# Four graph layers on one core: the closing algebra of layer 3 cut up by chunk, and artanh written as two logarithms

## The chip, the core and the metric

The kernel runs on one core of one Trainium2 chip. The metric is the device time of one execution in microseconds (us). The profiles below are taken from one execution each; in them PE is TensorE, DVE is VectorE, ACT is ScalarE, POOL is GpSimd and SP is SyncE.

## What is computed

Input `x` has 4096 nodes of 64 features, `adj` is a 4096 x 4096 matrix of zeros and ones. Four layers follow one another, each of the form x + layer(relu(layernorm(x)), adj). The change concerns the last layer, a graph layer in hyperbolic space:

```python
def _artanh(x):
    return jnp.arctanh(jnp.clip(x, -ARTANH_BOUND, ARTANH_BOUND))

def mobius_scalar_mul(r, x):
    x_norm = _norm(x)
    return _tanh(r * _artanh(x_norm)) * (x / x_norm)

def weighted_midpoint_lincomb(A, X):
    gamma = lambda_x(X)
    num = A @ (gamma * X)
    den = A @ (gamma - 1.0)
    sgn = jnp.where(den >= 0.0, 1.0, -1.0)
    den = sgn * jnp.maximum(jnp.abs(den), DEN_EPS)
    two_mean = num / den
    mid = mobius_scalar_mul(0.5, two_mean)
    alpha = jnp.sum(A, axis=1, keepdims=True)
    return mobius_scalar_mul(alpha, mid)

# layer 3: XW = mobius_matvec(W, h); AXW = weighted_midpoint_lincomb(A, XW)
#          x + expmap0(relu(logmap0(AXW)))
```

So after the large product with A, every node needs a sign, a length, an artanh, a tanh and a scaling of its 64 numbers.

## The kernel before

**Tiling.** The 4096 nodes are 32 blocks of 128. For layer 3 the output is made in 8 chunks (`u` = 0 to 7) of four blocks (CB = 4, 512 nodes). `sum3` (line 1674) runs the product for one chunk: for each of its four blocks, matmuls over the input blocks, each with 196 columns (65 numbers in three bf16 parts, and a column of ones). The sums lie in PSUM, for most chunks in two banks of two blocks each (pool `one`, four banks), for chunks 5 and 2 in one double bank (pool `two`).

**Order of layer 3.** `layer3` (line 1690) first sums what is available of the inputs: chunks 0, 1, 2 over the first half of the blocks, taken out into SBUF as `early`; then chunks 3, 4, 5 over the first half. When the last quarter of the inputs is there, it finishes chunks 3, 4, 5, then 0, 1, 2, and then makes 6 and 7 whole. After each chunk `take3` (line 1737) brings the sums out: ScalarE copies the first part and the column of ones (`alpha`), VectorE adds the two other parts, and for chunks 0 to 2 the `early` part. Then `summed` (line 1729) collects chunks: once three are together, or at once for the chunks 6 and 7 (`alone=True`), it hands them to `post3`.

**The closing algebra.** `post3` (line 1757) works on three chunks at a time, 12 numbers per partition in the small steps, or on one chunk with 4. It has two sections. The head, once for each chunk, takes the sign (`sgn`), multiplies the 256 numbers by it (written as `n` in the profile, from the tile's name `n65`), squares them on ScalarE (`sq`) and on VectorE (the positive part), makes `den` in two steps and reduces the squares to `ss`. The rest is for all chunks of the group together: `preload(AF.Ln)`, the reciprocal `rc` of `den`, the root in `lengths` (names `guess`, `nt`, `nu`, `ny`, `norm`), `t`, then `artanh2` (line 1595), the multiplication by `alpha`, tanh on ScalarE, and for each chunk a scaling of `n`, the addition to `X` and the output DMA, issued by SyncE.

**artanh2.** The argument is clipped (`axc`). VectorE makes 1 - x (`at`), its reciprocal (`rc`) and (1 + x) times that; ScalarE takes the logarithm, and `preload(AF.Tanh)`, an activation on a constant, brings in the table of tanh. Meanwhile VectorE evaluates a polynomial (`flow`, `x`, `po`) that replaces the logarithm for arguments under 0.25. `artanh2` is called four times by `post3` and four times by `pre3` (line 1621), which prepares the inputs of layer 3.

**What sets the order.** Each engine runs its instructions in the order in which the program issues them. The class `Weave` (line 605) decides that order when the program is built: it keeps a planned clock for each engine with estimated durations. Generators such as `post3` yield their VectorE (`DV`), ScalarE (`AC`) and SyncE (`SY`) steps; they lie in `weave.work`, and the first two of them are looked at (`width` is 2). `draw` (line 711), called after every fourth matmul in `sum3`, issues each VectorE or ScalarE step whose planned end lies no later than TensorE's planned time plus a margin (`LAG` 0.4 us and `late`, 1.0 us since layer 1), the first generator first. `fill` (line 692) does that ahead of an instruction of `take3`, which is issued directly. `force` issues whatever can begin first, and `finish`, after the last chunk, forces all that is left. Just before `finish`, `layer3` loads a register of each engine from the tile `flag`, by which a general program would run if the adjacency matrix were not made of zeros and ones.

**Buffers.** Small tiles (`stat`) share 22 buffers of 24 columns, those of up to 512 columns (`b2`) share 20.

Of the kernel before, what the change touches and what calls it, by code (L numbers as in the profile page):

```python
# [12 lines left out]
AF = mybir.ActivationFunctionType  # L13
ALU = mybir.AluOpType
AX = mybir.AxisListType
# [4 lines left out]
D = 64  # L20
# [9 lines left out]
DEN_EPS = 1e-10  # L30
# [541 lines left out]
CB = 4  # L572
# [219 lines left out]
def fast_kernel(ctx: ExitStack, tc: tile.TileContext, t: dict, out: bass.AP, flag: bass.AP):  # L792
# [24 lines left out]
    weave = Weave()  # L817
# [11 lines left out]
    def b2(name, shape=(P, QB, D), dtype=F32):  # L829
        return b2p.tile(list(shape), dtype, tag="b2", name=name)  # L830

    def stat(name, n):
        return small.tile([P, ST], F32, tag="st", name=name)[:, :n]
# [3 lines left out]
    DV, AC, GP, SY = (Engine(weave, x.e, x.real, True) for x in (V, S_, G_, Y_))  # L837
# [79 lines left out]
    def rows(s, width=D):  # L917
        return s[:, :, None].to_broadcast([P, s.shape[1], width])
# [12 lines left out]
    def recip(v):  # L931
        r = stat("rc", v.shape[1])
        yield DV.reciprocal(r, v)
        return r
# [160 lines left out]
    ones = const.tile([P, 1], F32, name="fones")  # L1095
# [483 lines left out]
    def lengths(s):  # L1579

        yield DV.tensor_scalar(s, s, NORM_EPS2, None, op0=ALU.max)
        r = yield from rsqrt(s)
        n = stat("norm", s.shape[1])
        yield DV.tensor_tensor(n, s, r, ALU.mult)
        return n, r
# [5 lines left out]
    def preload(func):  # L1591

        yield AC.activation(void, tab, func)

    def artanh2(x, between=()):

        nb = x.shape[1]
        xc = stat("axc", nb)
        yield DV.tensor_scalar(xc, x, ARTANH_BOUND, None, op0=ALU.min)
        r = stat("at", nb)  # L1600
        yield DV.tensor_scalar(r, xc, -1.0, 1.0, op0=ALU.mult, op1=ALU.add)
        q = yield from recip(r)
        yield DV.scalar_tensor_tensor(q, xc, 1.0, q, op0=ALU.add, op1=ALU.mult)
        yield AC.activation(q, q, AF.Ln)
        yield from preload(AF.Tanh)
        low = small.tile([P, ST], I32, tag="st", name="flow")[:, :nb]
        yield DV.tensor_scalar(low, xc, 0.25, None, op0=ALU.is_lt)
        x2, p = stat("x2", nb), stat("po", nb)
        yield DV.tensor_tensor(x2, xc, xc, ALU.mult)
        yield DV.tensor_scalar(p, x2, *(2.0 * c for c in ARTANH_POLY[:2]), op0=ALU.mult, op1=ALU.add)  # L1610
        yield DV.tensor_tensor(p, p, x2, ALU.mult)
        for c in ARTANH_POLY[2:-1]:
            yield DV.scalar_tensor_tensor(p, p, 2.0 * c, x2, op0=ALU.add, op1=ALU.mult)
        yield DV.scalar_tensor_tensor(p, p, 2.0 * ARTANH_POLY[-1], xc, op0=ALU.add, op1=ALU.mult)
        yield from between
        yield DV.copy_predicated(q, low, p)
        return q
# [3 lines left out]
    def pre3(q, kind):  # L1621
# [15 lines left out]
        mr, c = r[:, QB:], stat("ratio", QB)  # L1637
        yield DV.tensor_tensor(c, n[:, QB:], r[:, :QB], ALU.mult)
        a = yield from artanh2(n[:, :QB])
        yield DV.scalar_tensor_tensor(a, a, 0.5, c, op0=ALU.mult, op1=ALU.mult)  # L1640
        yield DV.tensor_scalar(a, a, TANH_CLAMP, None, op0=ALU.min)
# [48 lines left out]
    def layer3():  # L1690
# [21 lines left out]
        for place, u in enumerate(sets[1]):  # L1712
            sum3(u, place, half + QB if place < 2 else half, NB)
            summed(u, take3(u))
        for place, u in enumerate(sets[0]):
            sum3(u, place, half, NB)
            summed(u, take3(u, early.pop(u)))
        for place, u in enumerate((6, 7)):
            sum3(u, place, 0, NB)
            summed(u, take3(u), alone=True)  # L1720
# [3 lines left out]
        weave.finish()  # L1724
        return others

    group = []

    def summed(u, parts3, alone=False):
        group.append((u, parts3))  # L1730
        if alone or len(group) == 3:
            weave.add(post3(group[:]))
            group.clear()

    out_nm = out

# [17 lines left out]
            V.tensor_tensor(alpha, alpha, more[1], ALU.add)  # L1754
        return n65, alpha

    def post3(parts3):

        nb = CB * len(parts3)
        sgn, den, ss = stat("sgn", nb), stat("den", nb), stat("ss", 2 * nb)
        part = [slice(i * CB, (i + 1) * CB) for i in range(len(parts3))]
        vs = [n65[:, :, :D] for u, (n65, al) in parts3]
        for h, v, (u, (n65, al)) in zip(part, vs, parts3):
            d = n65[:, :, D]
            yield DV.tensor_scalar(sgn[:, h], d, 0.0, 2.0, op0=ALU.is_ge, op1=ALU.mult)
            yield DV.scalar_tensor_tensor(v, rows(sgn[:, h]), -1.0, v, op0=ALU.add, op1=ALU.mult)  # L1770
            sq = b2("sq")
            yield AC.activation(sq[:, :CB, :], v, AF.Square)
            yield DV.scalar_tensor_tensor(sq[:, CB:, :], v, 0.0, v, op0=ALU.max, op1=ALU.mult)
            yield DV.tensor_scalar(den[:, h], d, -1.0, DEN_EPS, op0=ALU.mult, op1=ALU.max)
            yield DV.tensor_tensor(den[:, h], den[:, h], d, ALU.max)
            yield DV.tensor_reduce(ss.rearrange("p (k b) -> p k b", k=2)[:, :, h],
                                   sq.rearrange("p (k b) d -> p k b d", k=2), AX.X, ALU.add)
        yield from preload(AF.Ln)
        rd = yield from recip(den)
        n, r = yield from lengths(ss)  # L1780
        t = stat("t", nb)
        yield DV.tensor_tensor(t, n[:, :nb], rd, ALU.mult)
        ratio = stat("ratio", nb)

        def between():
            yield DV.tensor_tensor(ratio, n[:, nb:], r[:, :nb], ALU.mult)

        a = yield from artanh2(t, between())
        for h, (u, (n65, al)) in zip(part, parts3):
            yield DV.scalar_tensor_tensor(a[:, h], a[:, h], 0.25, al, op0=ALU.mult, op1=ALU.mult)  # L1790
        yield DV.scalar_tensor_tensor(a, a, ARTANH_MAX, ratio, op0=ALU.min, op1=ALU.mult)
        yield AC.activation(a, a, AF.Tanh)
        yield DV.tensor_tensor(a, a, r[:, nb:], ALU.mult)
        for h, v, (u, (n65, al)) in zip(part, vs, parts3):
            yield DV.scalar_tensor_tensor(v, v, 0.0, rows(a[:, h]), op0=ALU.max, op1=ALU.mult)
            x = X[u // 2][:, (u % 2) * CB:(u % 2 + 1) * CB, :]
            yield DV.tensor_tensor(x, x, v, ALU.add)
            yield SY.dma_start(out_nm[:, u * CB:(u + 1) * CB, :], x)
# [103 lines left out]
```

## Time and profile before

| | us |
|---|---|
| median of 3 runs | 809.76 (808.28 to 809.77) |
| the profiled execution | 808.12 |
| its span, first to last instruction | 806.1 |

Mean granted clock of TensorE: 0.992. In stretches of layer 3's end, busy us of each engine:

| stretch | PE | DVE | ACT |
|---|---|---|---|
| 718.10 to 740.70 | 22.60 | 16.59 | 10.90 |
| 740.70 to 750.30 (sums of 3, 4, 5 end) | 9.60 | 2.33 | 1.40 |
| 750.30 to 766.60 (chunks 0, 1, 2) | 16.30 | 14.52 | 6.10 |
| 766.60 to 777.40 (chunk 6) | 10.80 | 10.01 | 3.41 |
| 777.40 to 788.30 (chunk 7) | 10.90 | 9.72 | 4.38 |
| 788.30 to 806.10 (after the last matmul) | 0.01 | 10.46 | 6.04 |

A line of the timeline gives start, duration, engine, line, operation, output and input by the program's names with their shapes, and how many instructions are merged in it; in brackets stands how long the engine was idle before, and what released it. All steps issued through `DV` and `AC` have the line of the helper, 781, so they are told apart by their names. Consecutive VectorE instructions overlap by up to 0.1 us, so the sum of durations is larger than the time they take.

### The profile page before, as it was taken

The numbers are of one execution on the slowest core, as the hardware profiler recorded it, in microseconds if no ns is written. First come the engines' busy times: TensorE is split into PE (matmuls) and PEld (weight loads), VectorE is DVE, ScalarE is ACT, GpSimd is POOL, SyncE is SP. The second block draws the span as 40 slices with busy tenths as digits, with TensorE's granted clock in tenths as the row PEclk, the third lists the DMA queues.
The fourth block names the chain that finished last, engine by engine and source line by source line (L and its number), as shares of the span: only waits on it lengthen the run. The fifth ranks groups of instructions, "written<-read, shape, count | busy, mean of one in ns | idle before, by whom it ended". The sixth has DMA issues, their size and how long they took to land. (4 is left out here: it accounts for less than half of the span.)

```text
span 806.1 us, 12128 instructions
## 1 busy us (share of the span) xinstructions
PE 772.6 (96%) x4494; PEld 360.1 (45%) x4494; DVE 635.6 (79%) x1429; ACT 397.8 (49%) x613; POOL 60.6 (8%) x125
## 2 busy tenths in 40 slices
PE   5999999999999999999999999999999999999991
PEld 2334444544443323333333333444444444599991
DVE  6886867877778798888888887878788777776696
ACT  5655555566556556667666664122220245444332
POOL 3332232231000000000000000000000000000000
PEclk9999999999999999999999999999999999999996
DMA  9999999999601032004022016597888600000010
GB/s 221 152 177 191 215 163 211 202 180 205 186 26 40 0 103 85 23 8 124 0 66 66 0 51 229 193 338 240 292 307 280 216 7 20 2 1 2 2 41 17
DMA packets 43955, 98.40 MB, mean 122 GB/s; under 512 B 5104, under 2 KB 20464, under 8 KB 43888
## 3 DMA queue, kind: packets, MB, share of 16 engines
q1 hardware_dynamic: 25888, 78.98, 29.0%
q0 software_dynamic: 15840, 14.42, 19.1%
q10 hardware_dynamic: 2160, 4.14, 1.4%
q8 instruction: 37, 0.61, 0.3%
q14 instruction: 30, 0.25, 0.1%
HBM read 135.54 MB, written 5.24 MB: 175 GB/s over the span
## 5 line engine op out<-in xcount | busy, mean ns | idle before, releaser
L781 ACT ACTIVATE sig<-score,fatt_add,fatt_mul 128x1024 f32<-128x1024 f32 x128 | 148.3, 1200 | 85.2 <-PE score L976 84.1
L781 DVE TENSOR_TENSOR sig<-sig,A 128x1024 f32<-128x1024 f32 x128 | 151.6, 1222 | 38.2 <-ACT sig L781 37.5
L781 DVE SCALAR_TENSOR_TENSOR whole<-whole 128x1024 f32<-128x1024 f32 x128 | 153.0, 1219 | 6.7 <-DMA whole<-in_adjT 6.1
L781 ACT ACTIVATE w<-cnt 128x512 int16<-128x512 f32 x198 | 111.6, 595 | 88.4 <-PE cnt L976 83.7
L976 PE MATMUL score<-qd,kT 64*128 64x512 f32 x512 | 128.2, 617 | 0.0
L976 PE MATMUL acc<-sig,S 128*64 128x512 f32 x512 | 125.4, 606 | 1.5 <-DVE sig L781 1.4
L976 PE MATMUL acc<-A,hm 128*128 128x512 fp8e4 x512 | 115.9, 379 | 0.0
L976 PEld LDWEIGHTS <-hm 128*128 128x128 bf16 x768 | 73.4, 98 | 91.3 <-issue 9.8
L976 PE MATMUL cnt<-A,ftri 128*128 128x512 fp8e4 x256 | 98.0, 386 | 8.1 <-ACT A L781 8.1
L976 PE MATMUL cnt<-A,fupd 128*128 128x512 fp8e4 x248 | 95.4, 385 | 3.4 <-ACT w L781 0.9
L976 PE MATMUL acc<-S,A 128*128 128x196 bf16 x1024 | 88.2, 246 | 0.2 <-DVE mx L781 0.2
L976 PEld LDWEIGHTS <-A 128*128 128x128 fp8e4 x1024 | 87.1, 96 | 1.5 <-issue 1.2
L976 PEld LDWEIGHTS score<-qd,kT 64*128 64x128 f32 x512 | 43.7, 186 | 80.9 <-ACT sig L781 39.1
L976 PE MATMUL acc<-w,hm 128*128 128x512 bf16 x256 | 75.6, 379 | 0.0
L781 DVE TENSOR_SCALAR w<-cnt 128x512 int16<-128x512 f32 x58 | 40.1, 691 | 39.4 <-PE cnt L976 38.2
L860 POOL DMA_DIRECT2D A<-in_adjT x110 | 58.8, 536 | 133.1 <-DMA A<-in_adjT 132.3
L976 PEld LDWEIGHTS acc<-sig,S 128*64 128x64 f32 x512 | 30.4, 136 | 82.7 <-issue 38.8
L976 PEld LDWEIGHTS <-lo 128*64 128x64 bf16 x768 | 39.3, 109 | 51.2 <-issue 22.5
L976 PE MATMUL acc<-A,lo 128*64 128x512 fp8e4 x512 | 59.4, 381 | 0.0
L781 ACT ACTIVATE mt<-acc 64x512 f32<-64x512 f32 x32 | 18.9, 591 | 66.0 <-PE acc L976 65.5
L976 PEld LDWEIGHTS <-ftri 128*128 128x128 bf16 x256 | 24.8, 98 | 47.2 <-issue 20.3
L1659 POOL MEMSET S<- 128x4 bf16 x8 | 0.9, 115 | 533.6 <-PE ps_l L976 463.2
(185 smaller groups left out, 631.5 us busy)
## 6 DMA issues: line engine op xcount, KB each, us to landing
whole<-in_adjT SPq DMA_DIRECT2D x128, 512.0 KB, 6.9
A<-in_adjT POOLq DMA_DIRECT2D x110, 128.0 KB, 14.0
qd<-qs SPq DMA_DIRECT2D x16, 128.0 KB, 4.1
mx<-gs SPq DMA_DIRECT2D x16, 128.0 KB, 7.8
xT<-gs SPq DMA_DIRECT2D x8, 256.0 KB, 7.2
x<-in_x SPq DMA_DIRECT2D x6, 256.0 KB, 6.2
xs<-x SPq DMA_DIRECT2D x4, 256.0 KB, 6.0
qs<-qT ACTq DMA_DIRECT2D x4, 256.0 KB, 6.0
```

What stands on the lines that cost most here:

```text
L781: return fn(*args, **kw)
L860: nc.gpsimd.dma_start(A8[q][b // 2][:, b % 2, :], a)
L976: nc.tensor.matmul(o, lhsT, rhs, start=start, stop=stop, skip_group_check=True)
L1659: nc.gpsimd.memset(S3[q, c][:, :, 3 * e:], 1.0)
```

## The change

`head3` takes the head out of `post3`. When the first or second chunk of a group of three has been summed, its head is given to the planner at once, with the tiles `sgn`, `den` and `ss` set up for the whole group. When the third arrives, whatever of the two heads is not issued yet is issued, and `post3` runs the third head and the rest. Chunks 6 and 7 run as before. In `artanh2` the two steps before the reciprocal's product and the reciprocal go; ScalarE takes ln(1 + x) and ln(1 - x), with the affine part in the activation, and VectorE subtracts.

```diff
@@ artanh2
-        r = stat("at", nb)
-        yield DV.tensor_scalar(r, xc, -1.0, 1.0, op0=ALU.mult, op1=ALU.add)
-        q = yield from recip(r)
-        yield DV.scalar_tensor_tensor(q, xc, 1.0, q, op0=ALU.add, op1=ALU.mult)
-        yield AC.activation(q, q, AF.Ln)
+        q, r = stat("at", nb), stat("ln", nb)
+        yield AC.activation(q, xc, AF.Ln, bias=ones)
+        yield AC.activation(r, xc, AF.Ln, bias=ones, scale=-1.0)
         yield from preload(AF.Tanh)
...
         for c in ARTANH_POLY[2:-1]:
             yield DV.scalar_tensor_tensor(p, p, 2.0 * c, x2, op0=ALU.add, op1=ALU.mult)
+        yield DV.tensor_tensor(q, q, r, ALU.subtract)
         yield DV.scalar_tensor_tensor(p, p, 2.0 * ARTANH_POLY[-1], xc, op0=ALU.add, op1=ALU.mult)
@@ summed
-    group = []
+    group, heads = [], []

     def summed(u, parts3, alone=False):
+        if not group:
+            n = CB if alone else 3 * CB
+            group.append((stat("sgn", n), stat("den", n), stat("ss", 2 * n)))
         group.append((u, parts3))
-        if alone or len(group) == 3:
-            weave.add(post3(group[:]))
-            group.clear()
+        i = len(group) - 2
+        if not alone and i < 2:
+            weave.add(head3(i, parts3, *group[0]))
+            heads.append(weave.work[-1])
+            return
+        for piece in heads:
+            while piece in weave.work:
+                weave.issue(piece)
+        heads.clear()
+        weave.add(post3(group[1:], *group[0]))
+        group.clear()
@@ post3
+    def head3(i, part3, sgn, den, ss):
+        h = slice(i * CB, (i + 1) * CB)
+        n65, al = part3
+        v, d = n65[:, :, :D], n65[:, :, D]
+        yield DV.tensor_scalar(sgn[:, h], d, 0.0, 2.0, op0=ALU.is_ge, op1=ALU.mult)
+        yield DV.scalar_tensor_tensor(v, rows(sgn[:, h]), -1.0, v, op0=ALU.add, op1=ALU.mult)
+        sq = b2("sq")
+        yield AC.activation(sq[:, :CB, :], v, AF.Square)
+        yield DV.scalar_tensor_tensor(sq[:, CB:, :], v, 0.0, v, op0=ALU.max, op1=ALU.mult)
+        yield DV.tensor_scalar(den[:, h], d, -1.0, DEN_EPS, op0=ALU.mult, op1=ALU.max)
+        yield DV.tensor_tensor(den[:, h], den[:, h], d, ALU.max)
+        yield DV.tensor_reduce(ss.rearrange("p (k b) -> p k b", k=2)[:, :, h],
+                               sq.rearrange("p (k b) d -> p k b d", k=2), AX.X, ALU.add)
...
-        for h, v, (u, (n65, al)) in zip(part, vs, parts3):
...
+        yield from head3(len(parts3) - 1, parts3[-1][1], sgn, den, ss)
```

More of the change, by code (lines that the diff above doesn't have):

```diff
@@ L1755, in take3, with post3 @@
         return n65, alpha
-    def post3(parts3):
+    def head3(i, part3, sgn, den, ss):
[11 more added lines that the diff above has]
+                               sq.rearrange("p (k b) d -> p k b d", k=2), AX.X, ALU.add)
+    def post3(parts3, sgn, den, ss):
         nb = CB * len(parts3)
-        sgn, den, ss = stat("sgn", nb), stat("den", nb), stat("ss", 2 * nb)
         part = [slice(i * CB, (i + 1) * CB) for i in range(len(parts3))]
         vs = [n65[:, :, :D] for u, (n65, al) in parts3]
-        for h, v, (u, (n65, al)) in zip(part, vs, parts3):
[L1768 to L1777, printed above, removed]
+        yield from head3(len(parts3) - 1, parts3[-1][1], sgn, den, ss)
         yield from preload(AF.Ln)
```

## The prediction, made before the changed kernel was run

> **What bounds the kernel now.** I read the timeline of TensorE first, since the page gives it 96% of the span, then the timelines of VectorE and ScalarE over the last 70 us, then what touches the tile `flag`.
>
> ```profile
> PE 772.6 (96%) x4494; PEld 360.1 (45%) x4494; DVE 635.6 (79%) x1429; ACT 397.8 (49%) x613; POOL 60.6 (8%) x125
> 718.11 70.20 PE L976 MATMUL acc<-S,A 128*128 128x196 bf16 x824
> ```
>
> From 718.11 to 788.31 TensorE runs the sums of layer 3 without a gap. The change touches none of those matmuls, so 788.31 stays. What can move is what follows: 788.31 to the last VectorE instruction at 800.71, then 5.4 us of output transfer and program end (806.1 less 800.71), which also stay.
>
> In the VectorE timeline the columns are start, duration, engine, line, operation, names and shapes, and in brackets the idle time before.
>
> ```profile
> 745.21 0.61 DVE L781 TENSOR_TENSOR n<-n,acc 128x130 f32<-128x130 f32 x2 [0.74 <-ACT alpha L781]
> 750.75 0.88 DVE L781 TENSOR_TENSOR n<-n,acc 128x260 f32<-128x260 f32 x2 [4.93 <-ACT alpha L781]
> ...
> 755.30 0.16 DVE L781 TENSOR_SCALAR sgn<-n 128x4 f32<-128x4 f32 x1
> ...
> 757.17 0.61 DVE L781 TENSOR_TENSOR n<-n,acc 128x130 f32<-128x130 f32 x2
> ...
> 774.86 0.22 DVE L781 RECIPROCAL rc<-den 128x12 f32<-128x12 f32 x1
> ```
>
> VectorE idles 4.93 us before the sum of chunk 5 arrives at 750.75, and from there has work almost to the end: it enters the last 50 us with a backlog. Closing algebra of chunks 3 and 4 could have been done in that gap, but waits for chunk 5. One head (from `sgn` to the reduction) takes 757.17 - 755.30 = 1.87 us.
>
> ```profile
> 788.94 0.61 DVE L781 TENSOR_TENSOR n<-n,acc 128x130 f32<-128x130 f32 x2
> 789.91 0.17 DVE L781 TENSOR_SCALAR flow<-axc 128x4 int32<-128x4 f32 x1 [0.36 <-issue]
> ...
> 791.71 0.16 DVE L781 TENSOR_SCALAR sgn<-n 128x4 f32<-128x4 f32 x1
> ...
> 794.45 0.17 DVE L781 RECIPROCAL rc<-den 128x4 f32<-128x4 f32 x1
> ...
> 796.78 0.17 DVE L781 TENSOR_SCALAR axc<-t 128x4 f32<-128x4 f32 x1
> 796.99 0.17 DVE L781 TENSOR_SCALAR at<-axc 128x4 f32<-128x4 f32 x1
> 797.19 0.18 DVE L781 RECIPROCAL rc<-at 128x4 f32<-128x4 f32 x1
> 797.40 0.16 DVE L781 SCALAR_TENSOR_TENSOR rc<-axc,rc 128x4 f32<-128x4 f32 x1
> 797.49 0.16 DVE L781 TENSOR_SCALAR flow<-axc 128x4 int32<-128x4 f32 x1
> ...
> 800.29 0.42 DVE L781 TENSOR_TENSOR X<-X,n 128x256 f32<-128x256 f32 x1
> ```
>
> The last chunk, 7, is added up by 789.55, but its `sgn` starts only at 791.71, since chunk 6 is still in work, and two big steps of chunk 6 stand inside its head: `sgn` to `rc` takes 794.45 - 791.71 = 2.74 us there, not 1.87. So the end is set by VectorE's backlog, over a floor: chunk 7's own chain after the last matmul.
>
> **What the Trainium skill says.** "ScalarE: Activation LUTs", What ACT_TABLE_LOAD costs: a table load is about 1283 ns, a pointer operand adds about 93 ns to an ACTIVATE, and neighbours overlap by about 93 ns. The trace agrees: loads here are 1.28 us, and a sigmoid of 512 columns from PSUM with a bias pointer takes 686 ns, a copy of that size 593. "VectorE: DVE Perf Modes", The DRAIN you can't avoid: the next instruction waits for the pipe to empty, and one that is not held starts earlier. Here dependent small steps start 0.20 us apart, independent ones 0.09 (797.40 to 797.49). "ScalarE: Activation LUTs", Table sets: cheap functions stand in every set. The squares at 769.89 and 782.82 run on the tanh table with no load before them, so earlier heads bring no table switch.
>
> **The change part by part.**
>
> *Heads at once.* For chunks 3, 4 and 0, 1 seven VectorE steps and one square move ahead. Nothing is added, and no DMA moves. Heads 3 and 4 cost 2 x 1.87 = 3.74 us of VectorE. They are ready at about 743.1 and 745.8 and fit before 750.75 even behind the adds of chunk 4; that gap hides them. Heads 0 and 1 move within a stretch in which VectorE is busy anyway: no gain, no loss. A head placed ahead of a take delays the release of PSUM banks; chunk 0's are last read at 760.2 and needed by chunk 6 at about 766.5, so that has 6 us of room, chunk 1's 12. Backlog saved: 3.74 us; if the planner leaves the gap unused, nothing.
>
> *artanh.* Per call `at`, the reciprocal and the product go; `flow` then follows `axc` after 0.20 us, at 796.98 instead of 797.49: 0.51 less. One subtraction is added. It depends on nothing that VectorE has just written, and stands between two dependent steps: 0.09 by the spacing above (0 to 0.20 as bounds). Net 0.42 per call. ScalarE gets two logarithms for one. A plain one takes 0.205 here; with the pointer 0.205 + 0.093 = 0.30 each, overlapped 0.51 for both. In chunk 7's old clock: first at 797.00, second done at 797.51, load to 798.81, preload of tanh from 798.83; tanh could begin at 798.94. VectorE delivers its operand at 799.36 - 0.42 = 798.94. A tie, so ScalarE costs nothing, up to 0.1 if the logarithms are longer. In the four calls of `pre3` TensorE is full; the last one's result is ready at 737.54, and its first matmul comes at about 739.3 (32 matmuls of 0.085 us before the second half of chunk 3 is copied at 742.1). Nothing there.
>
> *What is late next.* The backlog of the second group (0, 1, 2) starts at 774.86 - 3.74 - 0.42 = 770.70. That is above its floor: chunk 2's adds end at 768.6, and its head makes 770.2 at the earliest (old order). From 774.86 to 784.37 the old run needs 9.51 us, with 0.42 of chunk 6's head inside and 0.28 of small waits; less 0.42 for artanh that is 8.4 to 8.7, so it ends at about 779.3. Chunk 6 then takes 1.87 + (800.71 - 794.45 = 6.26) - 0.42 = 7.71 us: 787.0. Chunk 7 cannot start its adds before 788.73: its copy is at 788.35, and adds follow the copy's start by 0.38 everywhere before. So chunk 6 is out of the way, with 1.7 us to spare, 1.2 after the first half's adds; the end falls to the floor.
>
> *The floor.* Adds at 788.73, the second at 789.05. Then one wait that has lain on chunk 6's side comes onto chunk 7's: each engine loads the register from `flag` there, and VectorE's queue stands meanwhile.
>
> ```profile
> L1723 DVEq TENSOR_LOAD <-flag x1: 542/542/542, 789.3 to 789.3; - x1
> ```
>
> It started 0.04 after the last add (789.26), and `flow` came 0.07 after its end. So `sgn` starts at 789.05 + 0.04 + 0.54 + 0.07 = 789.70, and the end is 789.70 + 1.87 + 6.26 - 0.42 = 797.41. Against 800.71 that is 3.30 us: 2.01 from the earlier start, 0.87 from an undisturbed head, 0.42 from artanh. The profiled execution took 808.12 (span 806.1 and 2.0 around it): 804.8. The median of the runs shown, 809.76, lies 1.64 above that execution; taken off it, 806.5, which is what I name.
>
> **Rivals.**
>
> 1. *The gap stays empty* (the change does not do what it says): heads 3 and 4 are issued only when chunk 5 forces them. For it: order is fixed beforehand by a planner with estimated durations, at least 0.09 us for a matmul where the trace has 0.085. Against it: the planner is asked after every fourth matmul and then issues each step that fits. Only artanh is left, 4 x 0.42 = 1.7 us: 808.1.
> 2. *Chunk 6 ends late.* If interleaving leaves 1 to 2 us more than I count, its last steps again lie inside chunk 7's head: 1.0 to 2.3 us gained, 807.5 to 808.8. For it: the spare time is only 1.2 us.
> 3. *Slower: VectorE stands behind a square.* ScalarE's queue is in order. If the square of head 0 is queued behind the copies of chunk 1, which wait for TensorE until about 761.1, the reduction of head 0 holds VectorE from about 757.5, 4 us; the same with head 1 and chunk 2 (766.6), 3.5 us. 7.5 less the 5.4 saved (3.74 + 4 x 0.42) is 2.1 slower: 811.9. It decides once these stands exceed 5.4 us. For it: copies of the old run wait on TensorE up to 5.1 us. Against it: the square's input is ready 4 us before those copies, and the planner goes by readiness.
>
> **How the numbers follow.** Forecast 0.56, with 2.6 to 3.8 us gained (the 0.1 of the logarithms, the subtraction's bounds, the register load on or off the path): 806.0 to 807.2. Rival 2, 0.20; rival 1, 0.14; rival 3, 0.10. Runs of the same kernel differ by 1.5 us here, so 0.2% (1.6 us) is about what can be told from no change. The range takes the forecast less that scatter and rivals 1 and 2: 804.5 to 809.2. Faster: 0.54 of the forecast, 0.13 of rival 2 and 0.07 of rival 1 make 0.74; slower 0.09 of rival 3; the remaining 0.17 is within 0.2%.
>
> **What would show it.** The steps `sgn` of chunks 3 and 4 before 750; idle time before chunk 5's adds down from 4.93 to about 3 or less; the second group's `rc<-den` at about 770.7; chunk 6's last `X` before 788.7; `sgn` of chunk 7 near 789.7, right behind the register load; last `X` ending near 797.4; TensorE's end unmoved at 788.3. I am wrong if TensorE gets a gap after 718, if a square waits behind copies, or if chunk 6's steps still stand behind chunk 7's `sgn`.

## The result and the profile after

The changed kernel took 813.25 us in the median of 6 runs (812.21 to 814.48), the kernel before 808.14 (6 runs, 807.94 to 809.77): a ratio of 1.0055, interval 1.0043 to 1.0067, or about 4.4 us slower. Executions of either kernel fall into two groups 1.8 us apart, and since the kernels below have unequal shares of them, a ratio can be off by two or three tenths of a per cent, and fastest execution against fastest is given beside it where that matters (here 807.94 to 812.21, 4.3 us). The profiled execution of the changed kernel took 814.15 (span 812.2), that of before 808.12 (span 806.1): 1.8 us of the difference between the two traces is not the change's.

The close of the kernel went as forecast; TensorE came to it late. From the page, the timeline of TensorE and the register loads of the changed kernel:

```profile
PE 775.4 (95%) x4473; PEld 362.3 (45%) x4494; DVE 633.2 (78%) x1413; ACT 402.1 (50%) x623; POOL 61.8 (8%) x125
```

```profile
729.28 68.50 PE L976 MATMUL acc<-S,A 128*128 128x196 bf16 x804
```

```profile
L1722 DVEq TENSOR_LOAD <-flag x1: 544/544/544, 798.5 to 798.5; - x1
```

The last sum of layer 3 ends at 797.8 (729.28 + 68.50), not 788.3. The timeline of VectorE at the close:

```profile
752.61 0.17 DVE L781 TENSOR_SCALAR sgn<-n 128x4 f32<-128x4 f32 x1
...
755.66 0.17 DVE L781 TENSOR_SCALAR sgn<-n 128x4 f32<-128x4 f32 x1
...
760.29 0.88 DVE L781 TENSOR_TENSOR n<-n,acc 128x260 f32<-128x260 f32 x2 [2.67 <-ACT alpha L781]
...
796.41 0.43 DVE L781 TENSOR_TENSOR X<-X,n 128x256 f32<-128x256 f32 x1
796.75 0.61 DVE L781 TENSOR_TENSOR n<-n,acc 128x130 f32<-128x130 f32 x2
798.20 0.62 DVE L781 TENSOR_TENSOR n<-n,acc 128x130 f32<-128x130 f32 x2 [0.84 <-ACT alpha L781]
799.17 0.17 DVE L781 TENSOR_SCALAR sgn<-n 128x4 f32<-128x4 f32 x1 [0.36 <-DVE n L781]
...
806.37 0.42 DVE L781 TENSOR_TENSOR X<-X,n 128x256 f32<-128x256 f32 x1
```

Heads of chunks 3 and 4 now run before chunk 5 arrives (752.61 and 755.66), the idle time ahead of it is 2.67 us instead of 4.93, chunk 6 is finished before the last adds, and `sgn` of chunk 7 follows them with only the register load between (0.36 us idle). From TensorE's end to the last step it is 806.79 - 797.78 = 9.0 us; before it was 800.71 - 788.31 = 12.4. So 3.4 us were gained there.

They were lost, and more, ahead of the sums of layer 3, in layer 2, where the prediction expected nothing. There `pre3` runs beside the gates: matmuls `rz` and `ih`, a sigmoid `r` on ScalarE over the first half of `rz`, then the matmuls of its second half. TensorE's timeline of the changed kernel there:

```profile
675.33 1.02 PE L976 MATMUL rz<-mx,g 128*64 128x512 f32 x4
676.29 1.09 PE L976 MATMUL ih<-mx,g 64*64 64x512 f32 x8
677.31 0.66 PE L980 MATMUL ps_t<-fident,h 128*128 128x128 f32 x4
677.80 0.59 PE L976 MATMUL acc<-A,hm 128*128 128x512 fp8e4 x2
680.64 1.08 PE L976 MATMUL rz<-mx,g 128*64 128x512 f32 x4 [2.24 <-ACT r L781]
...
708.09 1.08 PE L976 MATMUL rz<-mx,g 128*64 128x512 f32 x4 [2.08 <-ACT r L781]
```

and ScalarE's, with the tanh that it ran before:

```profile
664.67 0.19 ACT L781 ACTIVATE at<-at 128x8 f32<-128x8 f32 x1
...
678.00 0.60 ACT L781 ACTIVATE h3T<-ps_t 128x512 f32<-128x512 f32 x1 [6.25 <-PE ps_t L980]
678.60 1.28 ACT L781 ACT_TABLE_LOAD   x1
679.90 0.69 ACT L781 ACTIVATE r<-rz,gate_b 128x512 f32<-128x512 f32 x1
...
705.41 0.63 ACT L781 ACTIVATE sq<-xc 128x512 f32<-128x512 f32 x1 [4.24 <-DVE xc L781]
706.05 1.28 ACT L781 ACT_TABLE_LOAD   x1
707.35 0.69 ACT L781 ACTIVATE r<-rz,gate_b 128x512 f32<-128x512 f32 x1
```

In the kernel before the same stretch reads, in the timeline of all engines:

```profile
674.52 1.09 PE L976 MATMUL ih<-mx,g 64*64 64x512 f32 x8
674.67 0.69 ACT L781 ACTIVATE r<-rz,gate_b 128x512 f32<-128x512 f32 x1 [1.69 <-PE rz L976]
...
675.54 1.08 PE L976 MATMUL rz<-mx,g 128*64 128x512 f32 x4
...
676.55 0.66 PE L980 MATMUL ps_t<-fident,h 128*128 128x128 f32 x4
```

The second group of gate matmuls (`rz`) has to wait until the sigmoid `r` has read the first. Before, the sigmoid runs beside the `ih` matmuls and TensorE goes on. In the changed kernel the transposes `ps_t` of `pre3` are ahead of that gate, their copy `h3T` is ahead of the sigmoid on ScalarE, and the sigmoid's table, which the first `pre3` had replaced by those of the logarithm and of tanh, is loaded only behind it: TensorE stands, that is, has nothing that its order lets it run, for 2.24 us. ScalarE itself had been idle for 6.25 us before that copy, although the first half of `rz` was done at 676.35: it keeps to the issued order. At 706 to 708 TensorE stands 2.08 us behind a square of the next `pre3` and a load.

The windows of the changed kernel show what follows. The columns are the window, its length, then busy time and instructions of TensorE, its weight loads, VectorE, ScalarE and GpSimd, then the granted clock of TensorE, the DMA share and GB/s:

```profile
680.00:682.00 2.00, 1.36 (x7) 0.55 (x8) 1.35 (x2) 0.58 (x1) 0.00 (x0) 1.00 0.00 0
682.00:684.00 2.00, 2.00 (x10) 1.46 (x9) 0.09 (x1) 0.54 (x2) 0.00 (x0) 0.50 0.00 0
684.00:686.00 2.00, 2.00 (x7) 0.78 (x6) 1.35 (x3) 2.00 (x5) 0.12 (x1) 0.65 0.00 0
686.00:688.00 2.00, 2.00 (x13) 0.86 (x13) 1.68 (x10) 1.97 (x3) 0.12 (x1) 1.00 0.00 0
...
708.00:710.00 2.00, 1.91 (x11) 1.05 (x12) 1.86 (x6) 0.72 (x2) 0.00 (x0) 0.83 0.00 0
710.00:712.00 2.00, 2.00 (x14) 1.86 (x13) 1.21 (x2) 0.72 (x1) 0.00 (x0) 0.50 0.00 0
712.00:714.00 2.00, 2.00 (x22) 1.94 (x21) 1.55 (x3) 0.00 (x0) 0.00 (x0) 0.82 0.03 8
```

After each stand the granted clock drops to half for about 3.4 us. Work lost by that is 2 x (0.50 + 0.35) = 1.7 us the first time and 2 x (0.17 + 0.50 + 0.18) = 1.7 the second. Together: 2.24 + 2.08 idle, less 0.25 that the kernel before had at 697, and 3.4 of half clock make 7.5 us lost; less 3.4 gained, 4.1 slower, near the measured 4.4. With the 1.8 us above, 7.5 also makes 9.3 of the 9.5 us by which TensorE ended later (797.78 against 788.31).

### The profile page after: what moved, and what is told of

Same layout as the page of the kernel before. It is cut to its first block, busy times and chain, and to the rows that moved or that the text cites. A ratio compares the mean times of both kernels' runs of the same rounds, so it can differ in the third digit from the quotient of the medians.

```text
span 812.2 us, 12093 instructions
## 1 busy us (share of the span) xinstructions
PE 775.4 (95%) x4473; PEld 362.3 (45%) x4494; DVE 633.2 (78%) x1413; ACT 402.1 (50%) x623; POOL 61.8 (8%) x125
## 4 chain that ended last, share of the span: by engine, by line
PE 88%; DVE 6%; ACT 2%; issue 1%; DMA 1%; SPq 0%; DVEq 0%; ACTq 0%
PE acc L976 54%; PE score L976 14%; PE cnt L976 13%; PE rz L976 2%; DVE sig L781 2%; PE ps_t L980 1%; PE ps_l L976 1%; DMA whole<-in_adjT 1%; DVE ss L781 1%; PE ps_kq L976 1%; PE ih L976 1%; ACT w L781 1%; DVE nt L781 1%; ACT sig L781 1%; DVE w L781 1%
## 5 line engine op out<-in xcount | busy, mean ns | idle before, releaser
L976 PE MATMUL acc<-S,A 128*128 128x196 bf16 x1024 | 90.0, 249 | 0.0
L976 PE MATMUL acc<-w,hm 128*128 128x512 bf16 x235 | 70.6, 379 | 0.9 <-issue 0.2
```

The source lines that it names most:

```text
L976: nc.tensor.matmul(o, lhsT, rhs, start=start, stop=stop, skip_group_check=True)
```

## The experiments

The theory: the shorter artanh in `pre3` makes the planner arrange TensorE and ScalarE anew around the gates of layer 2, and the new order makes TensorE stand. The rivals: the heads do harm, or the new instructions themselves take time that ScalarE doesn't have.

**Heads alone.** From the changed kernel:

```diff
     def artanh2(x, between=()):
-        q, r = stat("at", nb), stat("ln", nb)
-        yield AC.activation(q, xc, AF.Ln, bias=ones)
-        yield AC.activation(r, xc, AF.Ln, bias=ones, scale=-1.0)
+        r = stat("at", nb)
+        yield DV.tensor_scalar(r, xc, -1.0, 1.0, op0=ALU.mult, op1=ALU.add)
+        q = yield from recip(r)
+        yield DV.scalar_tensor_tensor(q, xc, 1.0, q, op0=ALU.add, op1=ALU.mult)
+        yield AC.activation(q, q, AF.Ln)
...
-        yield DV.tensor_tensor(q, q, r, ALU.subtract)
```

> Heads at once, artanh as it was everywhere. Theory (the shorter artanh in the preparation of layer 3 makes the planner set TensorE's and ScalarE's order anew, and TensorE stands there): TensorE's order is that of before, so no idle time over 0.3 us after 600 and its end at the place of before; only the closing gains, 2.0 to 3.0 us: ratio to before about 0.997. Rival (the heads are the harm, through buffers or the order they force): slower by about 4 us, ratio 1.005.

Measured: 806.97 us against 809.49, ratio 0.997 (0.9959 to 0.9982). TensorE's order is that of before, with 0.25 us idle after 600. From TensorE's end (788.08) to the last step (797.74) it is 9.66 us, so the heads alone shorten the close by 2.74. The heads are not the harm.

**artanh alone**: the new `artanh2` in the kernel before, `summed` and `post3` untouched.

```diff
-        r = stat("at", nb)
-        yield DV.tensor_scalar(r, xc, -1.0, 1.0, op0=ALU.mult, op1=ALU.add)
-        q = yield from recip(r)
-        yield DV.scalar_tensor_tensor(q, xc, 1.0, q, op0=ALU.add, op1=ALU.mult)
-        yield AC.activation(q, q, AF.Ln)
+        q, r = stat("at", nb), stat("ln", nb)
+        yield AC.activation(q, xc, AF.Ln, bias=ones)
+        yield AC.activation(r, xc, AF.Ln, bias=ones, scale=-1.0)
...
+        yield DV.tensor_tensor(q, q, r, ALU.subtract)
```

> New artanh everywhere, heads as before. Theory: the two idle times of 2.1 to 2.2 us before a gate matmul and the half clock behind each come back, 7.7 us lost, less 1.7 us of shorter algebra at the close: about 6 us slower, ratio 1.0074. Rival (heads): no idle time, 1.7 us faster, ratio 0.998.

Measured: 815.07 against 809.49, ratio 1.0071 (1.0049 to 1.0093). Both stands are back, in TensorE's timeline:

```profile
679.08 1.95 PE L976 MATMUL rz<-mx,g 128*64 128x512 f32 x4 [2.24 <-ACT r L781]
706.48 1.97 PE L976 MATMUL rz<-mx,g 128*64 128x512 f32 x4 [2.08 <-ACT r L781]
```

So the harm is artanh's. Of its two uses, the next two runs leave one in question.

**New instructions, old plan, in `pre3`.** The whole change, but the four calls of `pre3` book the old three VectorE steps and one logarithm; what is issued are the two logarithms and the subtraction. `pre3` calls a copy of `artanh2` for this, and the lines show how the copy differs.

```diff
+    def plan(e, dur, i, o, issue=None, table=None):
+        def run():
...
+            weave.book(e, dur + more, names(i), names(o))
+            return issue() if issue else None
+        return Op(e, dur, names(i), names(o), run)
...
-        yield AC.activation(q, xc, AF.Ln, bias=ones)
-        yield AC.activation(r, xc, AF.Ln, bias=ones, scale=-1.0)
+        for i, o in ((xc, r), (r, q), (q, q)):
+            yield plan("D", 0.19, i, o)
+        yield plan("A", 0.2 + 0.9e-3 * nb, q, q, logs, AF.Ln)
```

`logs` issues both logarithms; the subtraction is issued with the last step of the polynomial.

> All of the change, but in the four calls of the preparation the new artanh is booked in the planner with the steps and durations of the old one, so that TensorE's order is that of before; the instructions issued are the new ones. Theory (the order is the harm, not the instructions): TensorE without idle time, the whole gain at the close, 3.4 us faster, ratio 0.996. Rival (two logarithms with a pointer operand cost ScalarE the time that is missing, whatever the order): slower by about 4 us as the changed kernel, ratio 1.005.

Measured: 804.44 against 809.49, ratio 0.9939 (0.9923 to 0.9956); fastest against fastest it gains 3.4 us (807.84 to 804.39), the gain of the close. TensorE's matmuls are issued in the order of the kernel before, and it is busy all the time in these windows:

```profile
670.00:690.00 20.00, 20.00 (x122) 9.18 (x122) 14.38 (x53) 10.46 (x18) 0.23 (x2) 1.00 0.02 7
690.00:720.00 30.00, 30.00 (x293) 24.10 (x290) 20.97 (x56) 12.80 (x30) 0.23 (x2) 1.00 0.00 1
```

**Old instructions, new plan, in `pre3`.** The converse, again in a copy of `artanh2`: the old three VectorE steps and the logarithm are issued, while the planner is told two logarithms and a subtraction.

```diff
-        yield AC.activation(q, xc, AF.Ln, bias=ones)
-        yield AC.activation(r, xc, AF.Ln, bias=ones, scale=-1.0)
+        yield plan("A", 0.2 + 0.9e-3 * nb, xc, q, log, AF.Ln)
+        yield plan("A", 0.2 + 0.9e-3 * nb, xc, r, None, AF.Ln)
...
-        yield DV.tensor_tensor(q, q, r, ALU.subtract)
+        yield plan("D", 0.19, q, q)
```

`log` issues the four old instructions.

> All of the change, but in the four calls of the preparation the old instructions of artanh are issued (three VectorE steps and one logarithm) while the planner is told the steps of the new one, so that TensorE's order is that of the changed kernel. Theory (order): both idle times and the half clock are there, about 4 us slower than before, ratio 1.005. Rival (the instructions): no idle time, 3.4 us faster, ratio 0.996.

Measured: 812.45 against 809.49, ratio 1.0042 (1.0029 to 1.0054), with TensorE's matmuls in the order of the changed kernel and both stands:

```profile
680.54 1.08 PE L976 MATMUL rz<-mx,g 128*64 128x512 f32 x4 [2.24 <-ACT r L781]
707.98 1.08 PE L976 MATMUL rz<-mx,g 128*64 128x512 f32 x4 [2.08 <-ACT r L781]
```

These two settle it: the stands go with what the planner is told, to the hundredth of a microsecond, and not with the instructions. Which of its comparisons tipped was not traced, nor which difference in its books did it: per call there are two VectorE steps of 0.19 us less and one logarithm more.

**The new artanh in the close only.**

```diff
     def pre3(q, kind):
-        a = yield from artanh2(n[:, :QB])
+        a = yield from artanh_dve(n[:, :QB])
```

`artanh_dve` is the old function.

> Heads at once and the new artanh in the closing algebra only; the preparation of layer 3 keeps the old artanh. Theory (order set in the preparation): TensorE without idle time over 0.3 us after 600, close 9.0 us after its end instead of 12.4: 3.4 us faster, ratio 0.996. Rival (something in the close slows the sums of layer 3): slower than before.

Measured: 806.3 against 809.51, ratio 0.9953 (0.994 to 0.9967). TensorE's only idle time after 600 is the 0.25 us of before. From its end (790.23) to the last step (799.23) it is 9.0 us, as in the changed kernel, so the close has its whole gain without the new artanh in `pre3`.

**The table asked for early.** TensorE's order stays that of the changed kernel; only the load moves.

```diff
     def gates(q, step):
...
+        yield from preload(AF.Sigmoid)
         yield PE(mx, lambda: gate(rz, 0, 0), 0.9, [2, 2])
```

> The changed kernel with one activation more at the start of each gate piece, on a constant, that asks for the sigmoid's table; TensorE's order stays that of the changed kernel. Theory (TensorE stands because the sigmoid's table is loaded only when the sigmoid's turn comes, 1.28 us, on a queue that TensorE waits for): the two idle times shrink from 2.24 and 2.08 to about 0.9 and 0.8 us; if the shorter ones no longer bring the half clock, about 1.5 us are lost and 3.4 gained: ratio 0.998. Rival (the copy that is now in front of the sigmoid, not the table, is the wait): idle times stay near 2 us, ratio 1.005 as the changed kernel.

Measured: 807.21 against 809.51, ratio 0.9974 (0.9962 to 0.9987). The two places in TensorE's timeline, and the first in ScalarE's:

```profile
679.05 1.08 PE L976 MATMUL rz<-mx,g 128*64 128x512 f32 x4 [0.83 <-ACT r L781]
703.54 1.08 PE L976 MATMUL rz<-mx,g 128*64 128x512 f32 x4 [0.79 <-ACT r L781]
```

```profile
677.82 0.60 ACT L781 ACTIVATE h3T<-ps_t 128x512 f32<-128x512 f32 x1 [4.74 <-PE ps_t L980]
678.32 0.68 ACT L781 ACTIVATE r<-rz,gate_b 128x512 f32<-128x512 f32 x1
```

With the load out of the way the stands are 1.4 and 1.3 us shorter, and the windows of 2 us around both (676 to 686, 702 to 708) show a clock of 1.00. So of the 7.5 us lost the order alone makes 1.4 (0.83 + 0.79 less 0.25), the two loads 2.7, and the half clock behind the longer stands 3.4; 3.4 gained at the close less 1.4 is 2.0; the ratio says 2.1, fastest against fastest 1.6 (807.84 to 806.21).

**The planner counts loads when it chooses.** It added 1.3 us for a change of table to its books after it had chosen; now it adds it to the time at which the activation is held to begin. Each activation carries the number of its table (`op.table`) for this.

```diff
     def begin(self, op):
-        return max(self.t[op.e], self.ready(op.e, op.ins, op.outs, op.kinds))
+        more = 1.3 if op.table is not None and op.table != self.table else 0.0
+        return max(self.t[op.e], self.ready(op.e, op.ins, op.outs, op.kinds)) + more
```

> All of the change, and the planner counts 1.3 us for a table load when it asks when an activation can begin; it did so only in its books, after having chosen. Theory: with the load in view the planner does not put the sigmoid where TensorE waits for its load, no idle time of 2 us before a gate, ratio 0.996; the order of the whole kernel may change too, so other waits may come: up to 1.002. Rival (the planner's view of the table has nothing to do with it): the two idle times stay, ratio 1.005.

Measured: 804.19 against 809.51, ratio 0.9937 (0.9922 to 0.9952), with the whole change in. TensorE has no idle time of 0.2 us or more after 600. Its timeline has the gates together again, and ScalarE's the sigmoid ahead of the copy:

```profile
676.04 1.09 PE L981 MATMUL ih<-mx,g 64*64 64x512 f32 x8
677.06 1.08 PE L981 MATMUL rz<-mx,g 128*64 128x512 f32 x4
678.07 0.66 PE L985 MATMUL ps_t<-fident,h 128*128 128x128 f32 x4
```

```profile
676.19 0.69 ACT L783 ACTIVATE r<-rz,gate_b 128x512 f32<-128x512 f32 x1 [2.08 <-PE rz L981]
678.76 0.60 ACT L783 ACTIVATE h3T<-ps_t 128x512 f32<-128x512 f32 x1 [1.89 <-PE ps_t L985]
```

That the stands go is shown; that they go because the planner now sees their loads is not, for it does not see them. In its list `TABLES` sigmoid and tanh have the same number, and the last activation with a table before the loads at 678.60 and 706.05 was a tanh each time (664.67 and 692.48), so for these two sigmoids it counts no load, before the edit or with it. The chip ran one of 1.28 us for each. What the edit moves are the loads of the exponential, of the logarithm and of the tanh behind it, and with them the order from layer 0 on: the first transposes of `S`, at 97.58 in the changed kernel, come at 135.79 in this one. So this is another order, without the stands, and which decision took them away was not traced.

**The same planner in the kernel before**, the same edit on it, as a control.

> The kernel before, with nothing changed but that the planner counts the table load. Theory (it cures what the shorter artanh had upset, and in the kernel before there was little to cure, 0.25 us of idle time): ratio 0.999 to 1.001. Rival (that planner is worth some us by itself, and hides a loss that the change would still have): ratio under 0.997.

Measured: 808.95 against 809.45, ratio 0.9998 (0.9989 to 1.0006). By itself it is worth little: 0.4 us by the spans of the two traces (806.1 and 805.7), which the ratio does not tell from nothing. The rest of what it gives in the changed kernel is the loss that it takes away.

**The register load ahead of the last two chunks**, on the kernel with the new artanh in the close only.

```diff
+        while weave.back:
+            weave.force(True)
+        others = nc.values_load(flag)
         for place, u in enumerate((6, 7)):
...
-        while weave.back:
-            weave.force(True)
-        others = nc.values_load(flag)
         weave.finish()
```

> As the kernel with the new artanh in the close only, and the register is loaded from the flag before the sums of the last two chunks instead of after them. Theory (the load stands in VectorE's queue between the last adds and the last head): the 0.36 us idle before the last sgn goes, 0.4 us less than without, ratio about 0.995. Rival (the wait is not on the path, or the load costs the same at another place): no difference.

Measured: 805.7 against 809.51, ratio 0.9948 (0.9934 to 0.9961). The idle time before the last `sgn` is gone, and from TensorE's end (789.71) to the last step (798.38) it is 8.7 us instead of 9.0. The wait is on the path, but 0.3 us is less than the intervals of the two kernels tell apart.

**Planner and register load together**, both edits on the changed kernel.

> All of the change, the planner that counts the table load, and the register load ahead of the last two chunks. Theory: the gains add, 0.3 to 0.4 us less than with that planner alone, ratio about 0.993, no idle time over 0.3 us after 600. Rival (the register load costs the same elsewhere): as with that planner alone, 0.9937.

Measured: 804.0 against 809.45, ratio 0.9942 (0.9929 to 0.9954). The close takes 8.7 us here too (789.90 to 798.58), but the time is that of the planner alone within the intervals. The change with that planner beats both kernels. Fastest execution against fastest, it gains 3.7 us (807.84 to 804.13), 3.4 of them at the close, and 4.0 with the register load moved as well (807.75 to 803.74); the ratios, 0.9937 and 0.9942, say more (5.1 and 4.7 us) than the traces account for.

## Why the prediction was wrong

- **The step that failed** is the sentence on `pre3`: "In the four calls of `pre3` TensorE is full; the last one's result is ready at 737.54, and its first matmul comes at about 739.3 ... Nothing there." With it went "The change touches none of those matmuls, so 788.31 stays". It priced the edit in `pre3` by durations and by the room before its results are needed, and put the change of the issued order at nothing, although the text itself said that a planner with estimated durations fixes it. The new bookings of `pre3` moved TensorE's and ScalarE's order around the gates, at a cost of 7.5 us. The matmuls of layer 3 are the same, but they come later. The old plan with the new instructions is without the loss, the new plan with the old instructions has it.
- **The forecast of the close held.** Chunk 7's chain was to end 9.1 us after the last matmul (797.41 - 788.31); it ended 9.0 after it. Alone, the heads gave 2.74 us (2.01 + 0.87 were forecast), and artanh in the close 0.66 more (9.66 to 9.0; forecast 0.42). That the register load would come onto chunk 7's path was right too: 0.36 us idle, and 0.3 us less without it.
- **artanh's sizes.** A logarithm with a pointer takes 0.30 us, as estimated, and two take 0.48 (803.59 to 804.07) where 0.51 was estimated. The subtraction costs nothing in chunk 7: from the pair of polynomial steps before it to the next it is 0.39 us in the old run (798.15 to 798.54) and 0.39 in the new (804.26 to 804.65). So a whole 0.5 us went, not 0.42; the other 0.14 of the 0.66 is a `sgn` of chunk 7 that came 1.38 us after TensorE's end (791.61 - 790.23) instead of 1.52 (789.60 - 788.08). One reading was too broad: adds follow their copy by 0.38 only where half a chunk is copied; for chunk 5 it was 0.48 (750.27 to 750.75). The sum used it for a half only.
- **Of the rivals**, 1 and 2 did not come: the gap was used and chunk 6 was out of the way before the last adds. Rival 3 named the right kind of trouble, ScalarE's queue in order with a copy in front of what another engine waits for, at the wrong place and on the wrong engine: TensorE stood, in layer 2, and VectorE did not in the close. That it forecast a loss at all is therefore luck.
- **Of the signs to be watched**, TensorE's end told of the error: 797.8 instead of 788.3. The one that was to name the cause, a gap after 718, looked too late: the stands were at 678 and 706.
- **The Trainium skill** says in "ScalarE: Activation LUTs", Table sets: "Batch activation calls by set, not by function". The traces agree: logarithm, tanh and sigmoid take turns where `pre3` runs beside the gates, at 1.28 us a load, and two of these loads made 2.7 us of the stands. In the kernel before, a tanh right after a sigmoid ran with no load (677.74 and 678.30), while a sigmoid after the tanh that follows the logarithm needed one (671.70), so asking for the sigmoid's table where `pre3` now asks for that of tanh might save loads. No run tried it.

## What to carry to other kernels

Where a planner fixes the order from estimated durations, an edit that changes what a helper books can move every order decided after its first call; compare the issued order of every engine around each of its callers, not only around the one that was meant. A plan can only avoid what it holds: here it had no load between a tanh and a sigmoid, the chip ran one, and TensorE waited for it. And a stand of TensorE is to be priced with the clock behind it: 2.24 and 2.08 us of waiting cost 1.7 us more each.

## What was not expected of the hardware

In the traces of three kernels each of six stands of 2.24 or 2.08 us was followed by about 3.4 us at a granted clock of 0.50, which costs 1.7 us on top of the wait; after stands of 0.83 and 0.79 us it stayed at 1.00. The Trainium skill, "TensorE: Matmul & The Clock Gate", What's actually happening, gives an idle window of about 3.4 us before the clock is throttled to half, and about 3.4 us of work before it is released. The half and the time spent at it agree with these traces; the idle time does not, 2.1 us were enough. A wait of 1.79 us, at 289 to 291 in layer 1, lies between: in the kernel before the clock stays, in the changed one it falls, as these windows show, first before, then after:

```profile
292.00:294.00 2.00, 1.98 (x12) 0.94 (x11) 2.00 (x4) 1.37 (x3) 0.00 (x0) 1.00 0.15 10
294.00:296.00 2.00, 2.00 (x12) 0.49 (x8) 1.15 (x3) 1.98 (x2) 0.00 (x0) 1.00 0.73 214
```

```profile
292.00:294.00 2.00, 1.98 (x8) 1.02 (x10) 2.00 (x3) 1.17 (x2) 0.00 (x0) 0.72 0.04 8
294.00:296.00 2.00, 2.00 (x6) 0.35 (x2) 0.41 (x3) 1.20 (x1) 0.00 (x0) 0.50 0.75 188
```

This is what makes executions differ by 1.8 us. All twelve traces have that wait, at 1.78 or 1.79 us. In eight of them the clock falls behind it, and each of these is of an execution of the longer kind of its kernel; in the kernel before, in the heads alone and in the same planner on the kernel before it stays at 1.00, and these three are of the shorter kind. Nowhere else before 780 is the clock below 1.00 in a window of 2 us, but for those behind the stands. (In the twelfth, of artanh alone, it stays too, with executions at three levels, 813.4, 815.1 and 816.8; the profiled one is from the middle.) The mean clocks of the other executions say the same: 0.989 for those of the changed kernel at 812.2 to 812.4, 0.987 for those at 814.1 to 814.5, and 3.4 us at half clock in 812 are 0.002. So the length of a wait near 1.8 us does not decide whether the clock falls; what does is not shown. A stand above 2 us may also pass without: the execution of artanh alone at 813.41 has a mean clock of 0.989, where the profiled one with two drops has 0.987, which fits a single drop.
